# Turning rows by VectorE blocks and a way through DRAM, in place of TensorE transposes, in a kernel's last FFN

## The chip, the cores and the metric

The kernel runs on one core of a Trainium2 chip, as one program. A core has a matrix engine (TensorE, PE in the profile, with its weight loads PEld), three elementwise engines (VectorE = DVE, ScalarE = ACT, GpSimd = POOL), a queue engine (SyncE, SP) that issues most transfers, and 16 DMA engines that move data between HBM (device DRAM) and the on-chip memory SBUF, which has 128 partitions. TensorE writes its results to PSUM, eight banks of 128 x 512 float32 here. Each engine runs its own instructions in order and waits for the others by semaphores. The metric is the device time of one execution in microseconds (us); a kernel's time is the median of its runs.

## What is computed

Eight sequences of 512 rows with 512 features pass through four layers, each with a residual and a layer norm behind it: causal attention with 16 heads, a mixture of eight experts with two chosen for each row, attention with 8 heads over 2 groups of keys, and an FFN with integer weights. The change lies in that last FFN:

```python
def _L1_ffn_ref(x, wq_gate, s_gate, wq_up, s_up, wq_down, s_down):
    DIM = 512
    HID = 1408
    ZERO_POINT = 128.0

    def _qlinear(x, wq, scale):
        W = (wq.astype(jnp.float32) - ZERO_POINT) * scale[:, None]
        return jnp.einsum('bsd,hd->bsh', x, W)
    gate = _qlinear(x, wq_gate, s_gate)
    gate = jax.nn.silu(gate)
    up = _qlinear(x, wq_up, s_up)
    return _qlinear(gate * up, wq_down, s_down)
...
x = _layernorm(x + _L1_ffn_ref(x, L1_ffn_wq_gate, L1_ffn_s_gate, L1_ffn_wq_up, L1_ffn_s_up, L1_ffn_wq_down, L1_ffn_s_down), axis=-1)
```

For each sequence the FFN takes 512 x 512 rows to a hidden width of 1408 and back.

## The kernel before

The program runs the four layers one after the other; what follows is about the last, class `IntegerFfn`, and what surrounds it. P = 128 is the number of partitions, NB = 8 the number of sequences ("batches"), S = D = 512, NT = 4 tiles of 128 rows, ND = 4 tiles of 128 features, NHID = 11 chunks of 128 hidden features.

**Where the rows are.** `env.xs[b]` holds batch b in SBUF with the rows on the partitions: `[128, NT, 512]`, row 128 t + p on partition p of tile t. A matmul contracts over the partitions, so gate and up need the features there: x has to be turned. That is `split` (L1013). For feature tile c it turns four 128 x 128 squares by TensorE into one PSUM bank, `ps_xT` (L1022), ScalarE copies the bank to `x_high` in float32r, a type that TensorE takes in one pass and that keeps fewer bits (L1023), and VectorE subtracts that from the bank, which gives the rest, `x_low` (L1024). The two halves together stand for x. They lie in the pool `rows` for even batches and in the pool `work` for odd ones, one buffer each; so the halves of batch b + 2 take the room of batch b's.

**A chunk.** `hidden` (L1047) makes chunk c of a batch: 8 matmuls for the gate into `ps_g` and 8 for up into `ps_u` (L1055: 4 feature tiles, 2 halves), Silu by ScalarE (`sg`, L1058), product and scale by VectorE (`hT`, L1060), then the halves of hT: the copy `h_half` high by ScalarE (L1063) and the rest, `h_half` low, by VectorE (L1064). `out` (L1067) multiplies a chunk's halves by the down weights and adds it into four banks `ps_f` (L1069: 4 row tiles, 2 halves, 8 matmuls). `ps_g` and `ps_u` have two banks each, `ps_f` four: all eight. `ps_xT` takes a bank of `ps_g`.

**A batch.** `batch` (L1080) runs through the 11 chunks; behind chunk c's gate and up comes chunk c - 1's `out`, so that VectorE and ScalarE have the time of the next gate and up for their part. In chunks 2 to 5 it calls `split` for one feature tile each of the next batch:

```python
if not final and 2 <= c < 2 + ND:
    self.split(b + 1, c - 2, self.p_gu.tile([P, S], F32, tag="g", name="ps_xT"))
```

After chunk 10 `scaled` (L1072) applies the output scales (`y_ffn`, L1075) and the residual (L1076), and `layernorm` (L143) makes statistics (L148, L149), a power on GpSimd (L150, L151) and the normalised rows (L153), and stores them by four DMAs of 256 KB on SP (L156). The last batch ends by another way, `last_rows`.

Batch 0's rows are turned before that, inside the attention, whose plan calls `split` four times. `run` (L1026) opens the pools, loads and converts the rest of the integer weights (L980, L994, with a check of their size, L926), while batch 0 runs, and then runs the batches.

**What sets the order.** The attention's order is written by hand. In the FFN a scheduler orders each engine's instructions by priority and readiness; instructions may stand ahead of others that the source has earlier. At a batch's end, for instance, the next batch's gate and up stand ahead of parts of what the source puts first.

Of the kernel before, what the change touches and what calls it, by code (L numbers as in the profile page):

```python
# [18 lines left out]
P = 128  # L19
NB = 8  # L20
# [43 lines left out]
class Inputs:  # L64
# [3 lines left out]
    def __init__(self, *aps):  # L68
        for name, ap in zip(self.names, aps, strict=True):
            setattr(self, name, ap)  # L70


class Env:
# [928 lines left out]
class IntegerFfn:  # L1002
# [2 lines left out]

    HELD = 4

    def __init__(self, env, guard, weights, rows):
        self.env, self.nc, self.guard, self.weights, self.rows = env, env.nc, guard, weights, rows
        self.halves = {}  # L1010

    def split(self, b, c, ps):


        nc = self.nc
        if c == 0:
            pool = self.work if b % 2 else self.rows
            self.halves[b] = [pool.tile([P, ND, S], F32R, tag=f"rows{i}", name=f"x3_{part}")
                              for i, part in enumerate(("high", "low"))]
        high, low = self.halves[b]  # L1020
        for t in range(NT):
            nc.tensor.transpose(ps[:, ts(t, P)], self.env.xs[b][:, t, ts(c, P)], self.env.ident)  # L1022
        nc.scalar.copy(high[:, c, :], ps)  # L1023
        nc.vector.tensor_tensor(low[:, c, :], ps, high[:, c, :].bitcast(F32), ALU.subtract)  # L1024

    def run(self, held_out, last_norm):  # L1026
        tc, nc, weights = self.env.tc, self.nc, self.weights
        with ExitStack() as phase:
            self.work = phase.enter_context(tc.tile_pool(name="d_work", bufs=1))
            self.p_gu = phase.enter_context(tc.tile_pool(name="d_gu", bufs=2, space=PSUM))  # L1030
            self.p_o = phase.enter_context(tc.tile_pool(name="d_o", bufs=1, space=PSUM))
            weights.open(phase.enter_context(tc.tile_pool(name="d_weights", bufs=1)), 3 * NHID - weights.at)
            self.sd = self.work.tile([P, D], F32, name="sd")
            with tc.tile_pool(name="d_slots", bufs=1) as slots:
                while weights.at < 3 * NHID:
                    weights.load(slots, 4, 3 * NHID)
                    weights.convert()
                nc.sync.dma_start(out=self.sd, in_=self.env.ins.s_down.partition_broadcast(P))
            self.late = phase.enter_context(tc.tile_pool(name="d_late", bufs=self.HELD))
            for b in range(NB):  # L1040
                self.batch(b)
                if b == 0:
                    last_norm()
                    ps = self.p_gu.tile([1, 1], F32, tag="g", name="ps_held")
                    nc.scalar.dma_start(out=held_out, in_=self.guard.partitions_held(self.env.const, ps))

    def hidden(self, b, c, held):  # L1047

        nc, vec, work, weights = self.nc, self.env.vec, self.work, self.weights
        g = self.p_gu.tile([P, S], F32, tag="g", name="ps_g1")  # L1050
        u = self.p_gu.tile([P, S], F32, tag="u", name="ps_u1")
        for ps, w in ((g, weights(2 * c)), (u, weights(2 * c + 1))):
            for dc in range(ND):
                for i, x in enumerate(self.halves[b]):
                    nc.tensor.matmul(ps, lhsT=w[:, ts(dc, P)], rhs=x[:, dc, :],  # L1055
                                     start=(dc, i) == (0, 0), stop=(dc, i) == (ND - 1, 1))
        sg = work.tile([P, S], F32, tag="sg", name="sg1", bufs=2)
        nc.scalar.activation(sg, g, AF.Silu, scale=vec[:, V_SG + c : V_SG + c + 1])  # L1058
        hT = work.tile([P, S], F32, tag="hT", name="hT2", bufs=2)
        nc.vector.scalar_tensor_tensor(hT, u, vec[:, V_SU + c : V_SU + c + 1], sg, ALU.mult, ALU.mult)  # L1060
        high, low = (self.late.tile([P, S], F32R, tag=f"h{i}", name="h_late") if held else
                     work.tile([P, S], F32R, tag=f"h{i}", name="h_half", bufs=2) for i in range(2))
        nc.scalar.copy(high, hT)  # L1063
        nc.vector.tensor_tensor(low, hT, high.bitcast(F32), ALU.subtract)  # L1064
        return high, low

    def out(self, os, t, c, parts):  # L1067
        for i, h in enumerate(parts):
            self.nc.tensor.matmul(os[t], lhsT=h[:, ts(t, P)], rhs=self.weights(2 * NHID + c),  # L1069
                                  start=(c, i) == (0, 0), stop=(c, i) == (NHID - 1, 1))  # L1070
# [8 lines left out]
    def batch(self, b):  # L1079
        env, nc = self.env, self.nc  # L1080
        os = [self.p_o.tile([P, D], F32, tag=f"o{t}", name=f"ps_f{t}") for t in range(NT)]
        final = b == NB - 1
        hold = NHID - self.HELD if final else NHID
        parts = {}
        for c in range(NHID):
            parts[c] = self.hidden(b, c, c >= hold)
            if 0 < c <= hold:
                for t in range(NT):
                    self.out(os, t, c - 1, parts[c - 1])

            if not final and 2 <= c < 2 + ND:
                self.split(b + 1, c - 2, self.p_gu.tile([P, S], F32, tag="g", name="ps_xT"))
        if not final:
            for t in range(NT):
                self.out(os, t, NHID - 1, parts[NHID - 1])
            for t in range(NT):
                self.scaled(b, os, t)
            env.layernorm(b, env.ins.out[b])
            return

        order = [(t, c) for ts_ in ((0, 1), (2,), (3,)) for cs in (range(hold, NHID - 1), (NHID - 1,)) for t in ts_ for c in cs]
        for t, c in order:
            self.out(os, t, c, parts[c])
            if c == NHID - 1:
                self.last_rows(b, t, self.scaled(b, os, t))
# [587 lines left out]
def usual_pass(tc, ins, held_out):  # L1693
    nc = tc.nc
    with ExitStack() as ctx:
        env = Env(ctx, tc, ins)
        guard = Guard(env)
        keep = ctx.enter_context(tc.tile_pool(name="routed", bufs=1, side="right"))
        dram = ctx.enter_context(tc.tile_pool(name="routed_rows", bufs=1, space=bass.MemoryType.DRAM))
        with tc.tile_pool(name="a_mm", bufs=2, space=PSUM) as p_mm, ExitStack() as attn1_ctx:  # L1700
            with tc.tile_pool(name="routes", bufs=1, side="right") as routes, \
                    tc.tile_pool(name="experts", bufs=1, side="right") as pool, ExitStack() as tiles_ctx:
                experts = Experts(env, pool)
                router, tiles, tables = attention0(env, guard, keep, routes, experts, dram, p_mm, tiles_ctx)

                def load_rows(b):
                    rows = router.rows[S * b : S * (b + 1)]
                    nc.sync.dma_start(out=env.xs[b], in_=rows.rearrange("(t p) d -> p t d", p=P))

                env.open_stream(ctx, range(NB // 2))  # L1710
                rows = ctx.enter_context(tc.tile_pool(name="c_rows", bufs=1))
                own = attn1_ctx.enter_context(tc.tile_pool(name="c_own", bufs=1))
                attention = Attention1(env, guard, router, rows, own, p_mm)
                beside = {tiles.next + 6 * (b + 1): lambda b=b: load_rows(b) for b in range(NB // 2)}

                for i, piece in enumerate(attention.first_pieces()):
                    beside[E * NT + 4 + 2 * i] = piece
                with in_order(tc):
                    while tiles.next < tiles.n:
                        tiles.step()  # L1720
                        next(tables, None)
                        beside.pop(tiles.next, lambda: None)()
                assert not beside and next(tables, None) is None
                tiles.rare()
            env.open_stream(ctx, range(NB // 2, NB), side="right")
            for b in range(NB // 2, NB):
                load_rows(b)
            weights = IntegerWeights(env, guard)
            weights.open(ctx.enter_context(tc.tile_pool(name="c_weights", bufs=1, side="right")), weights.FIRST)
            ffn = IntegerFfn(env, guard, weights, rows)  # L1730
            last_norm = attention.run(weights, ffn.split)
        ffn.run(held_out, last_norm)

# [305 lines left out]
```

## Time and profile before

| | us |
|---|---|
| median of 3 runs | 2284.05 (2281.4 to 2284.93) |
| the profiled execution | 2286.21 |
| its span, first to last instruction | 2284.5 |
| last FFN, first gate matmul to the end | 1766.8 to 2284.5 |
| granted TensorE clock, mean over the span | 0.995 |
| transposes `ps_xT` (L1022), all batches | 128 of 272 ns, busy 19.2 |
| copies `x_high` (L1023) | 32 of 587 ns |
| subtractions `x_low` (L1024) | 32 of 689 ns |

The profile is of one execution. Engines are named PE, PEld, DVE, ACT, POOL and SP; L12 is line 12 of the kernel. A row of a group gives line, engine, operation, the output and the inputs by their names, shapes and the count, then the busy time of all and the mean of one in ns, then the idle time of that engine just before them and what ended it. The chain of waits goes back from the last instruction to whatever released it. Matmul durations overlap each other, since matmuls are pipelined; what a matmul costs on the path is the distance from start to start.

### The profile page before, as it was taken

What the parts mean: (1) busy time and instruction counts of PE and PEld (TensorE: products, weight loads), DVE (VectorE), ACT (ScalarE), POOL (GpSimd) and SP (SyncE); (2) the same over time, 40 slices, a digit from 0 to 9 for tenths busy, and PEclk for the clock granted to TensorE, in tenths of its full rate; (3) what the DMA queues carried; (4) which work ended last, traced back from release to release, by engine and by line L of the source; (5) the groups of instructions that cost most, each with busy time, mean ns of one, the idle gap of its engine ahead of it and who ended that gap; (6) DMA issues with size and microseconds to landing.
All of it is one profiled execution on the core that took longest, in us unless ns stands there. A gap on an engine that the chain in (4) does not pass through costs nothing. (4 is left out here: it accounts for less than half of the span.)

```text
span 2284.5 us, 24183 instructions
## 1 busy us (share of the span) xinstructions
PE 2238.4 (98%) x9430; PEld 1153.0 (50%) x9430; DVE 1242.0 (54%) x1976; ACT 648.2 (28%) x937; POOL 496.2 (22%) x489
## 2 busy tenths in 40 slices
PE   9999999999998999999999999999999999999997
PEld 3344444444443444444443334443343777887776
DVE  3457576566657433242216877787667544444443
ACT  2332322323323221111223323333332222222222
POOL 2232423313233241131115122322211000000000
PEclk9999999999999999999999999999999999999999
DMA  8010101101112224232224011100100100000000
GB/s 290 19 56 1 56 19 37 56 1 56 47 45 74 93 85 174 91 125 88 92 84 147 10 56 56 49 27 27 37 1 17 48 19 19 19 19 19 19 19 20
DMA packets 58444, 126.63 MB, mean 55 GB/s; under 512 B 6210, under 2 KB 6210, under 8 KB 58322
## 3 DMA queue, kind: packets, MB, share of 16 engines
q1 hardware_dynamic: 47040, 89.32, 11.1%
q0 software_dynamic: 10560, 34.61, 5.2%
q8 instruction: 77, 1.26, 0.2%
q10 hardware_dynamic: 722, 1.07, 0.1%
q14 instruction: 45, 0.37, 0.0%
HBM read 89.59 MB, written 35.39 MB: 55 GB/s over the span
## 5 line engine op out<-in xcount | busy, mean ns | idle before, releaser
L845 PE MATMUL ps_gu<-experts,xrT 128*128 128x512 f32 (+1 forms) x520 | 248.7, 601 | 0.0
L1268 ACT ACTIVATE p<-sc 128x2048 f32<-128x2048 f32 (+1 forms) x96 | 152.9, 1593 | 189.0 <-PE sc L1264 189.0
L1273 POOL TENSOR_SCALAR_AFFINE_SELECT p<-p 128x512 f32<-128x512 f32 x128 | 93.2, 743 | 380.1 <-ACT p L1268 374.0
L1060 DVE SCALAR_TENSOR_TENSOR hT<-ps_u,vec,sg 128x512 f32<-128x512 f32 x88 | 65.8, 748 | 198.4 <-PE ps_u L1055 198.4
L1069 PE MATMUL ps_f<-ffn_w,h_half 128*128 128x512 f32 x672 | 169.8, 393 | 1.6 <-DVE h_half L1064 1.1
L934 POOL TENSOR_TENSOR g_total<-g_total,r_inv 128x512 f32<-128x512 f32 x64 | 89.7, 1402 | 359.7 <-DVE r_inv L1617 283.3
L1617 DVE RECIPROCAL r_inv<-r_inv 128x512 f32<-128x512 f32 x32 | 106.9, 3339 | 97.5 <-ACT r_inv L931 97.5
L1587 ACT ACTIVATE p<-sc 128x1024 f32<-128x1024 f32 x128 | 124.0, 1021 | 125.9 <-PE sc L1584 125.9
L1296 DVE TENSOR_TENSOR p<-p 128x1536 f32<-128x1536 f32 (+2 forms) x96 | 129.2, 1345 | 38.7 <-POOL p L1273 21.7
L1069 PEld LDWEIGHTS ps_f<-ffn_w,h_half 128*128 128x128 f32 x672 | 124.3, 188 | 34.9 <-DVE h_half L1064 7.6
L1055 PE MATMUL ps_g<-x_high,ffn_w 128*128 128x512 f32 x352 | 141.0, 401 | 0.8 <-DVE x L1558 0.8
L848 DVE TENSOR_TENSOR h<-ps_gu,h 128x256 f32<-128x256 f32 x67 | 28.4, 423 | 205.6 <-ACT h L847 205.6
L1055 PE MATMUL ps_g<-x_low,ffn_w 128*128 128x512 f32 x352 | 139.0, 395 | 0.0
L1055 PE MATMUL ps_u<-x_low,ffn_w 128*128 128x512 f32 x352 | 138.8, 394 | 0.0
L1055 PE MATMUL ps_u<-x_high,ffn_w 128*128 128x512 f32 x352 | 138.6, 394 | 0.0
L862 PE MATMUL ps_y<-experts,hT 128*128 128x512 f32 (+1 forms) x272 | 127.9, 593 | 0.5 <-ACT hT L856 0.5
L1584 PE MATMUL sc<-qT,kT 64*128 64x512 f32 x512 | 127.2, 615 | 1.0 <-ACT qT L1505 0.7
L1200 PE MATMUL ps_q<-experts 128*128 128x512 f32 x256 | 121.2, 615 | 4.3 <-DMA experts<-in_xT 4.3
L845 PEld LDWEIGHTS ps_gu<-experts,xrT 128*128 128x128 f32 x520 | 89.6, 192 | 68.2 <-issue 68.1
L1606 PE MATMUL av<-p,v 128*64 128x512 f32 x512 | 123.7, 605 | 0.0
L1193 PE MATMUL ps_v<-experts 128*128 128x512 f32 x256 | 116.3, 602 | 2.1 <-DVE v L1195 2.1
L1552 PE MATMUL ps_o<-attn_out,aoT 128*128 128x512 f32 x256 | 117.3, 602 | 0.8 <-ACT r_inv L931 0.8
(256 smaller groups left out, 3532.3 us busy)
## 6 DMA issues: line engine op xcount, KB each, us to landing
results<-y SPq DMA_DIRECT2D x68, 256.0 KB, 2.0
x<-in_x SPq DMA_DIRECT2D x8, 1024.0 KB, 7.5
experts<-in_gate_up SPq DMA_DIRECT2D x8, 1024.0 KB, 11.7
rows<-x SPq DMA_DIRECT2D x32, 256.0 KB, 2.1
x<-rows SPq DMA_DIRECT2D x8, 1024.0 KB, 11.3
experts<-in_xT SPq DMA_DIRECT2D x7, 1024.0 KB, 5.5
out<-x SPq DMA_DIRECT2D x28, 256.0 KB, 2.3
ffn_i<-in_wq_ffn SPq DMA_DIRECT2D x11, 512.0 KB, 4.3
```

The source lines that it names most:

```text
L845: mm = nc.tensor.matmul(ps, lhsT=xT[:, c, :], rhs=self.weights(i, c), start=c == 0, stop=c == ND - 1)
L862: self.nc.tensor.matmul(ps, lhsT=hT[:, c, :], rhs=self.weights(i, ND + c), start=c == 0, stop=c == self.NI - 1)
L1055: nc.tensor.matmul(ps, lhsT=w[:, ts(dc, P)], rhs=x[:, dc, :], start=(dc, i) == (0, 0), stop=(dc, i) == (ND - 1, 1))
L1069: self.nc.tensor.matmul(os[t], lhsT=h[:, ts(t, P)], rhs=self.weights(2 * NHID + c), start=(c, i) == (0, 0), stop=(c, i) == (NHID - 1, 1))
L1193: nc.tensor.matmul(ps, lhsT=xts[b][:, c, ts(t, P)], rhs=wv[:, c, :], start=c == 0, stop=c == ND - 1)
L1200: nc.tensor.matmul(ps, lhsT=wq[:, g, ts(c, P)], rhs=xts[b][:, c, :], start=c == 0, stop=c == ND - 1)
L1268: nc.scalar.activation(p, sc[:, :, :width], AF.Exp, scale=scale)
L1296: nc.vector.tensor_tensor(total[:, :, P * kt :], total[:, :, P * kt :], p[:, :, at : at + w], ALU.add)
L1552: nc.tensor.matmul(ps, lhsT=state[b]["aoT"][:, c, ts(t, P)], rhs=w_out[:, c, :], start=c == 0, stop=c == ND - 1)
L1584: nc.tensor.matmul(sc[:, j, :], lhsT=st["kT"][hs, ts(kt, P)], rhs=st["qT"][g][hs, :], start=True, stop=True)
L1587: nc.scalar.activation(p, sc, AF.Exp, scale=scale)
L1606: nc.tensor.matmul(st["av"][HD * j : HD * (j + 1), :], lhsT=st["v"][:, kt, HD * j : HD * (j + 1)], rhs=p[:, j, :], start=kt == 0, stop=kt ...
```

## The change

In the last FFN the rows of batches 1 to 7 no longer go over TensorE. A new class `Turn` turns them in two steps. `blocks` has VectorE turn each square of 32 x 32 by itself, one instruction for a row tile of 128 x 512, from `xs` into `turned`. That leaves the squares themselves in the wrong partitions. `out` stores the tile to a DRAM buffer by four DMAs on SP, each from 32 partitions, with runs of 128 floats, so that the squares change places; `back` loads the buffer by one DMA of 1,024 KB, 8 KB on each partition. Both use the same SBUF tile `turned`, in a pool of one buffer. There are two DRAM buffers, for even and odd batches.

The rows' order along the free dimension then is (block of 32, tile, row in the block) in place of (tile, row). Gate, up, Silu and product run on columns in that order; the two instructions that make the halves of hT put them in order again, by reading hT through a permuted view (`by_tile`). Batch 0 is turned as before.

`split` is now `parts` for batches 1 to 7: the copy and the subtraction read `turned` in SBUF and not PSUM. In `batch`, chunks 0 to 3 call `blocks` for one row tile each of the next batch (the fourth also issues the five DMAs), chunks 6 to 9 call `parts`. The pool of the last batch's held halves, `late`, is opened only after the pool of `turned` is closed.

```diff
+class Turn:
+    N = P // 32
+
+    def __init__(self, env, dram, n, name):
+        self.nc, self.n = env.nc, n
+        self.dram = dram.tile([P, ND, self.N, n * 32], F32, name=name)
+
+    def blocks(self, room, t, x):
+        out = room.rearrange("p (j t c) -> p j t c", t=self.n, c=32)[:, :, t, :]
+        self.nc.vector.transpose(out, x.rearrange("p (j c) -> p j c", c=32))
+
+    def out(self, room):
+        for i in range(self.N):
+            src = room[32 * i : 32 * (i + 1), :].rearrange("r (k j f) -> r k j f", j=self.N, f=self.n * 32)
+            self.nc.sync.dma_start(out=self.dram.rearrange("(j r) k i f -> r k j i f", j=self.N)[:, :, :, i, :], in_=src)
+
+    def back(self, room):
+        self.nc.sync.dma_start(out=room, in_=self.dram.rearrange("p k i f -> p (k i f)"))
+
+    def by_tile(self, a, turned):
+        if turned:
+            return a.rearrange("p (i t c) -> p t i c", i=self.N, c=32)
+        return a.rearrange("p (t i c) -> p t i c", i=self.N, c=32)
...
 class IntegerFfn:
...
+        self.turns = [Turn(env, dram, NT, f"turned_{i}") for i in range(2)]
...
+    def room(self, b):
+        pool = self.work if b % 2 else self.rows
+        self.halves[b] = [pool.tile([P, ND, S], F32R, tag=f"rows{i}", name=f"x3_{part}")
+                          for i, part in enumerate(("high", "low"))]
+
+    def blocks(self, b, t):
+        if t == 0:
+            self.room(b)
+            self.turned = self.raw.tile([P, ND * S], F32, tag="turned", name="turned")
+        turn = self.turns[b % 2]
+        turn.blocks(self.turned, t, self.env.xs[b][:, t, :])
+        if t == NT - 1:
+            turn.out(self.turned)
+            turn.back(self.turned)
+
+    def parts(self, b, c):
+        high, low = (half[:, c, :] for half in self.halves[b])
+        x = self.turned[:, ts(c, S)]
+        self.nc.scalar.copy(high, x)
+        self.nc.vector.tensor_tensor(low, x, high.bitcast(F32), ALU.subtract)
...
+            with tc.tile_pool(name="d_raw", bufs=1) as self.raw:
+                for b in range(NB - 1):
+                    self.batch(b)
...
             self.late = phase.enter_context(tc.tile_pool(name="d_late", bufs=self.HELD))
...
+            self.batch(NB - 1)
...
-        nc.scalar.copy(high, hT)
-        nc.vector.tensor_tensor(low, hT, high.bitcast(F32), ALU.subtract)
+        hT, *halves = [self.turns[0].by_tile(a, back) if b else a for a, back in ((hT, True), (high, False), (low, False))]
+        nc.scalar.copy(halves[0], hT)
+        nc.vector.tensor_tensor(halves[1], hT, halves[0].bitcast(F32), ALU.subtract)
...
-            if not final and 2 <= c < 2 + ND:
-                self.split(b + 1, c - 2, self.p_gu.tile([P, S], F32, tag="g", name="ps_xT"))
+            if not final and c < NT:
+                self.blocks(b + 1, c)
+            if not final and 0 <= c - 6 < ND:
+                self.parts(b + 1, c - 6)
```

More of the change, by code (lines that the diff above doesn't have):

```diff
@@ L1006, with __init__ @@
     HELD = 4
-    def __init__(self, env, guard, weights, rows):
+    def __init__(self, env, guard, weights, rows, dram):
         self.env, self.nc, self.guard, self.weights, self.rows = env, env.nc, guard, weights, rows
         self.halves = {}
+        self.turns = [Turn(env, dram, NT, f"turned_{i}") for i in range(2)]
[17 more added lines that the diff above has]
+        self.nc.vector.tensor_tensor(low, x, high.bitcast(F32), ALU.subtract)
     def split(self, b, c, ps):
@@ L1016, in split @@
         if c == 0:
-            pool = self.work if b % 2 else self.rows
-            self.halves[b] = [pool.tile([P, ND, S], F32R, tag=f"rows{i}", name=f"x3_{part}")
-                              for i, part in enumerate(("high", "low"))]
+            self.room(b)
         high, low = self.halves[b]
@@ L1038, in run @@
                 nc.sync.dma_start(out=self.sd, in_=self.env.ins.s_down.partition_broadcast(P))
-            self.late = phase.enter_context(tc.tile_pool(name="d_late", bufs=self.HELD))
[L1040 to L1045, printed above, removed]
+            with tc.tile_pool(name="d_raw", bufs=1) as self.raw:
+                for b in range(NB - 1):
+                    self.batch(b)
+                    if b == 0:
+                        last_norm()
+                        ps = self.p_gu.tile([1, 1], F32, tag="g", name="ps_held")
+                        nc.scalar.dma_start(out=held_out, in_=self.guard.partitions_held(self.env.const, ps))
+            self.late = phase.enter_context(tc.tile_pool(name="d_late", bufs=self.HELD))
+            self.batch(NB - 1)
     def hidden(self, b, c, held):
@@ L1729, in usual_pass @@
             weights.open(ctx.enter_context(tc.tile_pool(name="c_weights", bufs=1, side="right")), weights.FIRST)
-            ffn = IntegerFfn(env, guard, weights, rows)
+            ffn = IntegerFfn(env, guard, weights, rows, dram)
             last_norm = attention.run(weights, ffn.split)
```

## The prediction

> **What bounds the kernel now.** I read the busy shares first, then the stretches of the last FFN, one batch each, then the chain of waits inside one batch, then the costliest groups, the waits and the DMA rows.
>
> The page's busy shares:
>
> ```profile
> PE 2238.4 (98%) x9430; PEld 1153.0 (50%) x9430; DVE 1242.0 (54%) x1976; ACT 648.2 (28%) x937; POOL 496.2 (22%) x489
> ```
>
> Two stretches of the last FFN (time, busy time of each engine, granted clock, DMA share):
>
> ```profile
> core 0: us, PE busy (x) PEld busy (x) DVE busy (x) ACT busy (x) POOL busy (x), PEclk, DMA share, GB/s
> 1894.00:1958.00 64.00, 63.81 (x284) 51.31 (x283) 28.38 (x48) 16.77 (x26) 1.27 (x2) 1.00 0.05 17
> 1958.00:2021.00 63.00, 62.82 (x280) 50.53 (x279) 27.43 (x47) 16.77 (x26) 1.27 (x2) 1.00 0.05 17
> ```
>
> TensorE, 98% busy over the span, is busy for all but 0.2 us of each stretch, at full granted clock; VectorE is busy 44%, ScalarE 26%, the DMA engines 5%. So time taken from TensorE's stream is time off the end, as long as nothing else in a batch comes to exceed it.
>
> The chain of waits from batch 4 (counted from 0) into the next (start, length, what):
>
> ```profile
> 2021.44 1.88 PE ps_g L1055 x8
> ...
> 2034.94 1.81 PE ps_f L1069 x8
> 2036.75 0.44 PE ps_xT L1022 x4
> 2037.19 1.85 PE ps_g L1055 x8
> 2039.04 1.86 PE ps_u L1055 x8
> 2040.90 1.82 PE ps_f L1069 x8
> 2042.72 0.44 PE ps_xT L1022 x4
> ...
> 2060.62 1.87 PE ps_g L1055 x8
> 2062.49 1.86 PE ps_u L1055 x8
> 2064.35 1.82 PE ps_f L1069 x8
> 2066.17 1.87 PE ps_g L1055 x8
> ...
> 2084.82 1.88 PE ps_g L1055 x8
> ```
>
> The transposes stand on the path. A chunk with them takes 2043.15 - 2037.19 = 5.96 us (2043.15 is the end of the second group), one without 2066.17 - 2060.62 = 5.55. A batch takes 2084.82 - 2021.44 = 63.4.
>
> **The change, part by part.** *Removed from TensorE:* 16 transposes in each of seven batches, in 28 groups of four. A group is 0.44 by the chain, 0.41 to 0.42 by the difference of chunks; I take 0.43: 28 x 0.43 = **12.0 us**. Their matmul row (272 ns each, modelled ends) would give 30; those overlap, so the chain decides. Batch 0's four groups still go over TensorE, inside the attention.
>
> The rows that price what moves (busy, mean ns | idle before):
>
> ```profile
> L1060 DVE SCALAR_TENSOR_TENSOR hT<-ps_u,vec,sg 128x512 f32<-128x512 f32 x88 | 65.8, 748 | 198.4 <-PE ps_u L1055 198.4
> L1064 DVE TENSOR_TENSOR h_half<-hT,h_half 128x512 fp32r<-128x512 f32 x84 | 57.5, 691 | 46.1 <-ACT h_half L1063 46.1
> L1063 ACT CAST h_half<-hT 128x512 fp32r<-128x512 f32 x84 | 52.1, 621 | 154.0 <-DVE hT L1060 154.0
> ```
>
> *Halves of x.* Still four copies and four subtractions a batch, now from SBUF: as L1063 and L1064, 0.62 and 0.69 us (from PSUM 0.587 and 0.689). No change of load.
>
> *Block transposes.* Four of 128x512 a batch on VectorE. No row shows this operation. Bounds: 0.48 us (L153, four in 1.92) and 3.34 (the reciprocal, L1617, the dearest VectorE operation of this size). It has one input, one output and no arithmetic, so it is nearest to the simple ones: I take 0.69, 2.8 us a batch. The cover is VectorE's idle 35 us in 63; in one chunk of 5.55 it has 1.44 of its own work. In the built order they stand in most batches after chunk 2's hT, two ahead of chunk 2's low half and two behind it. That half is due some 4.6 us after hT; two blocks and the half take 2.1. Batch 0 is tightest: integers are converted there, the four blocks stand before chunk 4's hT and follow a conversion that waits for its load until 1789.48 and a reduction. I work out the low half ready at about 1796.8 against 1797.5 due. Nothing is lost; at double the price 2 us.
>
> The Trainium skill (VectorE: DVE Perf Modes, Rules for kernel authors) says to turn 128x128 on TensorE wherever PSUM will do, which speaks against this change, and in The three transpose paths gives 311 ns for VectorE's blocks of 128x128 bf16. Four of those would be 1.24 us a tile, an estimate; by it the sum would be about 10 us of gain in place of 12. No run so far shows the operation.
>
> *The way through DRAM.* Five DMAs a batch on SP: four writes of 256 KB, each from 32 partitions in runs of 512 B, then a load of 1,024 KB that waits for all four. Rows near and far (KB each, us from issue to landing):
>
> ```profile
> x<-rows SPq DMA_DIRECT2D x8, 1024.0 KB, 11.3
> out<-x SPq DMA_DIRECT2D x28, 256.0 KB, 2.3
> ffn_i<-in_wq_ffn SPq DMA_DIRECT2D x2, 1024.0 KB, 5.3
> attn_out<-in_w_attn SPq DMA_DIRECT2D x2, 512.0 KB, 17.4
> ```
>
> Packets of 2,048 B on this queue last 84 ns (median of the trace's packet records). The writes are 2,048 packets, 128 on each of 16 engines: 2.7 us if a quarter of the bytes takes a quarter of the time, 10.8 if a packet costs the same whatever its size; with 2.3 for a landing, 5 to 13. The load takes 5.3 to 11.3. Round trip 10 to 25 us; I take 16. The far bound is the row from 64 partitions: 2 x 17.4 + 11.3 = 46.
>
> Who waits for it: the copies x_high on ScalarE, behind them that chunk's h_half, behind that ps_f on TensorE. The lead, by the built order: rows of batches 3 to 7 are turned two batches ahead, at chunk 2, and split after chunk 10's gate and up (the halves' room is then free): seven chunks, 39 us. Batch 1's are turned before chunk 4 of batch 0 and split after chunk 8's Silu: 18 us, and 4 more before TensorE lacks anything. Batch 2's are turned after chunk 8 of batch 0 and split after chunk 2's Silu of batch 1: 20 us, under 1 of grace. At 16 all is hidden. On SP the load's wait holds back only the 256 KB writes of finished rows, for which nobody waits.
>
> *Between batches.* Here an edit isn't free. In batches 1 to 5 three x_high (1.86 us) now stand ahead of chunk 10's h_half on ScalarE, three x_low ahead of its low half on VectorE. Today the stretch from chunk 9's ps_f to chunk 1's loses 0.78 us by the timeline: 16 ps_f in 3.95 in place of 3.64, 0.35 in ps_u, 0.12 in the next ps_f. In the built order two gate matmuls (0.47) stand before the ps_f that needs the high half: it comes 2.75 us after chunk 9's ps_f begins, is due after 2.29, and a weight load comes first: a stall of 0.6. The low half is in time. ps_f then ends late, so the VectorE chain behind it (y_ffn, x, statistics, norm, chunk 0's low half) moves by 1.5 us; the built order asks for that half some 1.4 us later than before, leaving 0.1. So 0.7 in place of 0.8: nothing. Bounds: -0.8 a boundary, and +1.3 if the moved chain isn't absorbed, over five boundaries -4 to +6.5.
>
> *Permuted reads.* Columns of seven batches come in another order, and L1063's copy and L1064's subtraction put them right by reading hT in runs of 32. No row shows such a read; bounds once and twice the price. I take once: as many elements, one pass. Within a batch either is covered by 3 us of slack between the low half and its ps_f.
>
> **Sum.** The profiled execution took 2286.21 us (span 2284.5 and 1.7 around it), 2.2 above the median of the runs, 2284.05. 2286.2 - 12.0 = 2274.2 for it; on the median **2272**.
>
> **The rivals.**
> 1. *The first two turns land late.* At a round trip of 25 us the first costs 3 and the second 4: 2279. For: short runs, 32 partitions. Against: DMA engines at 5% and four 256 KB writes landing in 2.7 us together (packets from 1968.02 to 1970.76). 0.09.
> 2. *The turn through DRAM is slower than its lead; slower than before.* Beyond 22 us each microsecond costs up to two (both early turns), so from 27 us the 12 are gone, from 30 the kernel is measurably slower, and beyond 39 every batch stalls. At the far bound of 46: 24 + 25 + 5 x 7 = 84, 2356; at 35 us, 2299. For: the attn_out row. Against: that row and x<-rows wait behind other traffic in a busier part; here the queue is idle. 0.06. The Trainium skill (VectorE: DVE Perf Modes, The three transpose paths) warns that a plain DMA with strides for a transpose is 19 times slower than the crossbar's when the innermost stride is large; here the innermost run is 512 B in one piece, so by its own condition it would not apply. No run so far shows it.
> 3. *Permuted reads cost double.* 0.62 and 0.69 more on h_half's two steps: between batches, where there is no slack, the first ps_f waits 1.2, the chain behind moves on, 2.35 lost in place of 0.7: 1.65 x 7 = 11.5, 2283.5, no change. For: runs of 128 B. Against: nothing in the page. 0.07.
> 4. *Blocks at 3.34 us:* 13.4 a batch in two bursts. Two blocks ahead of the low half make ps_f wait 2.9, the next two 3.3, in five batches 31; in batch 0, 10 and 8: 49 lost, 2321. 0.04.
> 5. *More than 12:* the stalls between batches vanish (-4): 2268. 0.04.
>
> **How the numbers follow.** The forecast has 0.70, own range 2269 to 2277. Measured changes below 0.2% (4.6 us) can't be told from none, so faster means under 2279.5, slower over 2288.6. Faster: forecast 0.70, rival 5 0.04, half of rival 1 0.04: 0.78. Same: the other half 0.05 and rival 3 0.07: 0.12. Slower: rivals 2 and 4: 0.10. The range 2266 to 2283.5 reaches over rivals 5, 1 and 3 and leaves out 2 and 4 and the edges.
>
> **What would show it.** Right: no ps_xT after batch 0's; chunks of 5.55 us throughout; batches of about 61.7; 28 block transposes near 0.7 us; the load landed well before x_high. Wrong: ScalarE or VectorE waiting for the load of turned (rivals 1, 2, worst at the first two); L1063's and L1064's successors above 0.7 (rival 3); ps_f waiting for h_half over 1 us between batches.

## The result and the profile after

| | before | after |
|---|---|---|
| median, us | 2282.77 (2281.4 to 2284.93, 4 runs) | 2269.44 (2267.03 to 2271.88, 4 runs) |
| profiled execution and its span, us | 2286.21, 2284.5 | 2270.12, 2268.4 |
| last FFN, first gate matmul to the end | 1766.78 to 2284.49: 517.72 | 1764.29 to 2268.36: 504.08 |
| from one batch to the next, batches 3 to 6 | 63.38 to 63.39 | 61.34 to 61.39 |

The ratio is 0.9941, 95% interval 0.9924 to 0.9958: 13.3 us faster. Within the two traces the last FFN alone is 517.72 - 504.08 = 13.64 us shorter. It begins 2.5 us earlier as well, but its start lay anywhere from 1761.3 to 1767.6 us in the traces of this study. So I read the stage by itself.

Busy shares of the changed kernel:

```profile
PE 2224.5 (98%) x9318; PEld 1142.3 (50%) x9318; DVE 1257.6 (55%) x2004; ACT 645.4 (28%) x937; POOL 494.5 (22%) x489
```

TensorE has 112 matmuls fewer, VectorE 28 instructions more. A stretch of the last FFN, about one batch (time, busy time of each engine, granted clock, DMA share):

```profile
1886.00:1948.00 62.00, 62.00 (x269) 49.76 (x267) 30.13 (x52) 17.05 (x29) 1.26 (x2) 1.00 0.16 51
```

The DMA share is 0.16 in place of 0.05, and TensorE has no idle time left that shows here. Groups of the last FFN (busy us, mean ns of one | idle before, and what ended it):

```profile
L1122 DVE TENSOR_TENSOR h_half<-hT,h_half 128x512 fp32r<-128x512 f32 x84 | 57.3, 688 | 37.1 <-ACT h_half L1121 37.1
L1121 ACT CAST h_half<-hT 128x512 fp32r<-128x512 f32 x84 | 52.1, 620 | 147.5 <-DVE hT L1116 147.5
...
L88 DVE STREAM_TRANSPOSE turned<-x 128x512 f32<-128x512 f32 x28 | 17.8, 682 | 0.0
L1066 ACT CAST x_high<-turned 128x512 fp32r<-128x512 f32 x28 | 15.9, 618 | 4.2 <-PE ps_u L1111 4.2
```

A block transpose of 128x512 float32 takes 682 ns. The halves of hT, which now read runs of 32, cost what they did (688 against 691, 620 against 621; batch 0's eleven chunks, read in plain order, take 688 and 621, the other batches 686 to 691 and 619 to 621). ScalarE's copies never waited for the load of `turned`: what ended their idle time is `ps_u`.

The DMA rows (KB each, us from issue to landing) and SP's timeline over batch 0 (start, length, what):

```profile
turned<-turned SPq DMA_DIRECT2D x28, 256.0 KB, 3.9
turned<-turned SPq DMA_DIRECT2D x7, 1024.0 KB, 4.8
```

```profile
1791.72 3.25 SPq L93 DMA_DIRECT2D turned<-turned  x4
1798.33 0.36 SPq L96 DMA_DIRECT2D turned<-turned  x1
1817.53 3.22 SPq L93 DMA_DIRECT2D turned<-turned  x4
1824.14 0.34 SPq L96 DMA_DIRECT2D turned<-turned  x1
```

From the first write's issue to the load's is 6.6 us, and the load takes 4.8: a round trip of 11.4. The copies that use it began at 1810.69 and 1838.07, 19.0 and 20.5 us after the first write; for later batches it is 39 to 41.

The chain of waits from batch 2 into batch 3 (start, length, what):

```profile
by line: PE ps_f L1127 35.6%; PE ps_u L1111 32.7%; PE ps_g L1111 32.2%
...
1946.05 1.82 PE ps_f L1127 x8
1947.87 0.47 PE ps_g L1111 x2
1948.34 0.95 PE ps_f L1127 x4
1949.29 0.24 PE ps_g L1111
1949.53 1.03 PE ps_f L1127 x4
1950.56 1.17 PE ps_g L1111 x5
```

In this window, from 1944 to 2012 us, nothing but TensorE stands on the chain. Before, the same stretch between two batches ran over `y_ffn`, the statistics, the power on GpSimd and the normalisation; this is the kernel before from batch 3 into batch 4:

```profile
2017.49 3.95 PE ps_f L1069 x16
2021.44 1.88 PE ps_g L1055 x8
2023.33 0.68 DVE y_ffn L1075
...
2030.00 1.92 DVE x L153 x4
2031.92 0.61 DVE h_half L1064
2032.58 1.20 PE ps_f L1069 x4
```

Chunk 10's ps_f is now split, and gate matmuls of the next batch stand in the gaps.

Between batches 3 and 6 a batch takes 2.03 us less. Four groups of transposes at 0.43 are 1.7 of that; the remaining 0.3 is what the stretch between batches lost before and no longer loses. Over 28 groups and five boundaries that is 12.0 + 1.6, the 13.6 of the stage. This split is by subtraction. Adding up what the starts of matmuls around a boundary lie apart beyond their usual 230 ns (where it is over 245) gives 0.75 us before and 0.34 after, so 0.4 a boundary and 2.1 in all; the two ways differ by half a microsecond, and nothing here says which is nearer.

The other periods can't be compared one by one: 64.26, 63.40 and 63.40 before, 62.58, 59.50 and 63.49 after, for batches 0, 1 and 6. At the boundaries into batches 1 and 7 the changed kernel has the order of before, with all sixteen ps_f ahead of the next gate, and loses 0.73 and 0.75 as before. At the five between them, eight ps_f (1.8 us) come after the next batch's first gate matmul, so batch 1's period is short by them and batch 6's long.

### The profile page after: what moved, and what is told of

Read it like the earlier page. It is cut to its first block, busy times and chain, and to the rows that moved or that the text cites. A ratio compares the mean times of both kernels' runs of the same rounds, so it can differ in the third digit from the quotient of the medians.

```text
span 2268.4 us, 24071 instructions
## 1 busy us (share of the span) xinstructions
PE 2224.5 (98%) x9318; PEld 1142.3 (50%) x9318; DVE 1257.6 (55%) x2004; ACT 645.4 (28%) x937; POOL 494.5 (22%) x489
## 3 DMA queue, kind: packets, MB, share of 16 engines
q1 hardware_dynamic: 62832, 104.01, 13.6%
```

## The experiments

Stage means the last FFN from its first gate matmul to the end, in one trace. Medians are compared with runs of the kernel before on the same chip; those were 2283.4 us in the first four runs, 2284.58 in the next four, 2285.43 in the next three and 2286.05 beside the last.

### What a group of transposes costs

```diff
-        for t in range(NT):
+        for t in [*range(NT)] * (2 if b else 1):
             nc.tensor.transpose(ps[:, ts(t, P)], self.env.xs[b][:, t, ts(c, P)], self.env.ident)
```

> The kernel before, with each of the 28 groups of four TensorE transposes of batches 1 to 7 done twice into the same PSUM tile. Theory (a group costs the path its own 0.43 us, 12.0 us in all): 2294 to 2296 us, against 2282.8 before. Rival (the groups partly filled idle time of TensorE, and the gain came from elsewhere): 2290 us or less.

Measured: 2297.92 us, ratio 1.0060 (1.0046 to 1.0073), 14.5 us more than before and 1.9 above the range. The stage is 530.54 us, 12.8 more, and a batch 65.23 in place of 63.38, 1.85 for four groups: 0.46 a group. In the chunk differences of the kernel before it was 0.41. So a group costs 0.41 to 0.46 us in the chunks where it stands, none of it fills a gap, and 28 of them are 11.5 to 12.9 us. The stage is the cleaner number of the two: nothing was changed ahead of it, and what comes ahead of it differs from execution to execution by more than the 1.7 us between 14.5 and 12.8.

### What the turn costs while it is hidden

The block transposes and all DMAs are taken out; the halves read the rows as they lie.

```diff
-            self.turned = self.raw.tile([P, ND * S], F32, tag="turned", name="turned")
-        turn = self.turns[b % 2]
-        turn.blocks(self.turned, t, self.env.xs[b][:, t, :])
-        if t == NT - 1:
-            turn.out(self.turned)
-            turn.back(self.turned)
...
-        x = self.turned[:, ts(c, S)]
+        x = self.env.xs[b][:, c, :]
```

> The changed kernel without the whole turn: no block transposes on VectorE, no writes to DRAM and no loads back; the copies and subtracts that make the halves of x read the rows of batches 1 to 7 as they lie, so the rows of those batches enter the last FFN unturned. TensorE's instructions are the changed kernel's. Theory (28 block transposes of 0.68 us and seven round trips of 11.4 us lie wholly beside TensorE's work): the changed kernel's time within 1.5 us, 2268 to 2271 us, with periods of 61.3 us between batches as there. Rival (the hidden work costs something after all, through VectorE's 19 us or through a DMA share of 0.17 in place of 0.05): faster than the changed kernel by 3 us or more, 2266 us or less.

Measured: 2266.35 us (2264.29 to 2270.83), ratio 0.9930 (0.9917 to 0.9944). The median lies 1.65 below the theory's range and close to the rival's bound; by times alone it decides nothing, since the interval overlaps the changed kernel's. The stage does: 503.13 us, 0.95 less than the changed kernel's 504.08, and all of it is in the first two batches, 59.76 + 61.12 in place of 62.58 + 59.50. From batch 2 on the periods are 61.35 to 61.39, against 61.34 to 61.39. There the turn is free. In batch 0 the two kernels also differ in order: without the load to wait for, batch 1's copies are made as the FFN starts, and two normalisations no longer stand ahead of hT of chunk 0. So the 0.95 is not the turn's price. Most of it goes with the order: the kernel further down that turns batch 0 as well keeps every block and transfer and has 59.66 + 60.93 there, with only some 0.4 of the difference due to faster matmuls of two chunks (see there).

### The stretch between batches

As the run before, and `halves[b]` is batch 0's for all batches, so copies and subtracts go as well:

```diff
-            self.room(b)
...
+            self.halves[b] = self.halves[0]
...
-            if not final and 0 <= c - 6 < ND:
-                self.parts(b + 1, c - 6)
```

> The kernel of the run without the turn, and without the copies and subtracts that make the halves of x in batches 1 to 7 as well: all eight batches read batch 0's halves. The order that is built then has, between two batches, the sixteen matmuls of chunk 11's ps_f in a row, as before the change, and no gate matmuls of the next batch among them. Theory (of the 13.3 us gained, 12.0 are TensorE's own transposes, and the rest are stalls between batches that shrank from 0.78 to 0.4 us because gate matmuls of the next batch stand among those of ps_f): the stalls come back, 0.7 us in place of 0.4 at each of five boundaries, 1.5 to 2.5 us slower than the run without the turn: 2270 to 2272.5 us. Rival (the boundary got shorter because the TensorE transposes left it, and the order is nothing; or ScalarE's and VectorE's copies and subtracts, 1.3 us a tile, cost something): equal to the run without the turn, or faster, 2269.5 us or less.

Measured: 2272.18 us, ratio 0.9948 (0.9934 to 0.9961): 5.8 us slower than the run without the turn, with less work, where I had expected 1.5 to 2.5. The single runs of the two touch (2270.28 to 2272.89 against 2264.29 to 2270.83), so the stage is the surer number: 506.22, 3.1 more, and the periods 61.71 in place of 61.36. The rival falls. The chain of that kernel from batch 2 into batch 3:

```profile
1947.03 1.66 PE ps_f L1121 x6
1948.69 1.88 PE ps_g L1105 x8
...
1950.58 0.68 DVE y_ffn L1127
...
1957.25 1.92 DVE x L185 x4
1959.17 0.61 DVE h_half L1116
...
1959.83 1.20 PE ps_f L1121 x4
```

That is the chain of the kernel before again, through `y_ffn` and the normalisation to the low half that the first ps_f of the next batch waits for. The 0.35 us that a boundary loses more comes with that order and goes with the other one. No run changes only the order. But two boundaries of the same kernels bear it out: the one into batch 7 has the order of before in the changed kernel and loses what it lost (0.75), and the one into batch 1, which has the new order in the run without the turn and in the kernel that turns batch 0 too, loses 0.23 there in place of 0.73. The rest of the 5.8 us is not in the stage, and is not explained.

### The changed kernel again

> The changed kernel as it is, for a time from the same chip as the three runs beside it, and for a second look at what varies between executions. Theory (the stage of the last FFN, from its first gate matmul to the end, is set by TensorE's own work, and what differs between executions lies ahead of it): that stage 503.5 to 504.6 us again (504.08 in the first trace), the time 2267 to 2272 us. Rival (the stage itself varies by a microsecond or more): a stage outside 503 to 505 us; the 0.95 us by which the run without the turn was shorter there would then say nothing.

Measured: 2271.13 us (2269.6 to 2272.85), ratio 0.9942 (0.9929 to 0.9955); stage 504.33.

> The changed kernel once more, beside the two runs of this call: 2268 to 2272 us, its last stage 503.5 to 504.6 us, as in both traces so far (504.08 and 504.33).

Measured: 2272.35 us, just above the range, ratio 0.9938 (0.9925 to 0.9951); stage 504.03. Three traces of the stage agree within 0.3 us, while its start varies from 1764.3 to 1767.6. The ratios agree within 0.0004.

### A slower block transpose

```diff
-        turn.blocks(self.turned, t, self.env.xs[b][:, t, :])
+        for _ in range(5):
+            turn.blocks(self.turned, t, self.env.xs[b][:, t, :])
```

> The changed kernel with each block transpose done five times over into the same place, 5 x 0.68 = 3.4 us a tile, which is the upper bound of the prediction for one. VectorE gets 28 x 4 x 0.68 = 76 us more in the last FFN, where it is idle for more than 30 us of each batch's 61 us; the built order has twenty in a row behind chunk 3 of batch 0, and spreads the others over the chunks. Theory (hidden where VectorE has room within its chunk; the twenty in a row, 13.6 us, are paid but for the 2.7 us that four took and a chunk's slack): 8 to 11 us more than the changed kernel, all in batch 0, periods of 61.3 to 62 us afterwards: 2276 to 2283 us. Rival, as the prediction priced tiles of 3.34 us: 49 us more than its forecast, 2321 us. Rival (wholly hidden): within 2 us of the changed kernel.

Measured: 2275.76 us (2272.55 to 2277.44), ratio 0.9960 (0.9946 to 0.9974), 4.6 us more than the changed kernel beside it, half of what I had expected; stage 509.09, 4.8 more. The periods are 65.34, 62.54, 62.43, 60.52, 60.36, 61.35, 63.51. VectorE's timeline in batch 0 (start, length, what):

```profile
1790.35 11.97 DVE L88 STREAM_TRANSPOSE turned<-x 128x512 f32<-128x512 f32 x20
1802.25 1.36 DVE L1117 SCALAR_TENSOR_TENSOR hT<-ps_u,vec,sg 128x512 f32<-128x512 f32 x2
```

Twenty in a row hold VectorE for 12 us, and two chunks' hT come together behind them. TensorE has the gate matmuls of two chunks in a row meanwhile, sixteen of them, and so waits only 3.2 us of the 12. Another 1.7 are lost behind the wait: from 1803.0 to 1807.2 the granted clock is 0.59 on average, and the first matmuls start 427 ns apart. In all, 76 us of added VectorE work cost 4.8. These are five short instructions that others can come between, not one long one as in rival 4.

### A longer way through DRAM

The write and the load are done twice, and in another run four times:

```diff
-            turn.out(self.turned)
-            turn.back(self.turned)
+            for _ in range(2):
+                turn.out(self.turned)
+                turn.back(self.turned)
```

> The changed kernel with the write to DRAM and the load back done twice for each batch, one after the other; after an even number the rows of batches 1 to 7 stand in another order, so the last FFN gets them unturned. The way through DRAM then takes 2 x 11.4 = 22.8 us. The order that is built has the copies of the halves of batch 1 at the end of batch 0 and those of later batches ever later, with leads of some 39 us from the first write to the copy. Theory (the way is hidden as long as it is shorter than its lead, and twice the DMA traffic, a share of 0.3 in place of 0.17, costs TensorE nothing): the changed kernel's time within 2 us, 2268 to 2272 us; the copies wait for no load. Rival (DRAM traffic in itself slows TensorE's stage, or the copies wait): 2275 us or more, with waits for the load ahead of the copies.

Measured: 2279.76 us, ratio 0.9978 (0.9968 to 0.9988), 8.6 more than the changed kernel beside it; stage 511.61, 7.5 more (less 504.08). The theory's time fell, and the rival's cause is not what happened. The second load was issued at 1809.20 and the copies began at 1822.67, behind chunk 10's `h_half` and not behind a load; the period of batch 1 alone is 67.96, of batches 4 and 5 60.55 and 60.36. One stretch there, and what TensorE waited for between 1790 and 1850 us (total us, times, longest):

```profile
2077.00:2137.00 60.00, 60.00 (x260) 48.37 (x259) 28.09 (x49) 15.13 (x25) 1.27 (x2) 1.00 0.28 88
```

```profile
PEld ps_g L1112 <- DVE x_low L1068: 4.7, 1, 4.7
```

With a DMA share of 0.28 TensorE is busy without a gap in this stretch, so the traffic costs it nothing there. By the starts of matmuls, 6.4 of the 7.5 us are one boundary, where the order built for this kernel put batch 1's four subtractions on VectorE behind `y_ffn`, the residual and a statistic, and the first gate matmuls of batch 1 wait for them: 4.4 us of waiting, and 1.5 more because the next seven start some 427 ns apart and not 230, at a granted clock of 0.52 (1830.2 to 1833.3). At the three boundaries after it, the order of before is back and loses 0.72 to 0.75 each.

> As the run with two ways through DRAM, with four, 46 us in all, the far bound of the prediction; the rows stand in another order again. The order that is built has the copies and subtracts for batch 1 after chunk 10 of batch 0, and for every batch right ahead of its first gate matmul, behind the four y_ffn and the normalisation on VectorE. Theory (a late turn costs what TensorE waits for its last half of x, and no more): batch 1's load lands at 1791.7 + 46 = 1838 us, 11 to 12 us after its first gate matmul is due, and each of the other six boundaries costs 3 to 7 us, since four subtracts of 0.69 us stand behind VectorE's four y_ffn of 0.7 us there: 30 to 54 us together, 2300 to 2324 us. Rival, as the prediction priced it (each batch's copies stand in ScalarE's order 39 us behind the write and every one of seven waits): 2356 us. Rival (no cost, since the planner moves the copies): under 2280 us.

Measured: 2415.76 us, ratio 1.0582 (1.0566 to 1.0599); stage 646.33, 142 more. All three forecasts were far too low. Periods are 79.5 to 90.2 us. SP's timeline at one boundary, and SP's waits over the stage (total us, times, longest):

```profile
2051.23 3.22 SPq L93 DMA_DIRECT2D turned<-turned  x4
2084.00 1.55 SPq L188 DMA_DIRECT2D out<-x  x3
2085.72 0.46 SPq L96 DMA_DIRECT2D turned<-turned  x1
```

```profile
SPq L188 <- DVE x L185: 194.6, 9, 30.9
```

The chain there (start, length, what):

```profile
2085.72 6.16 DMA turned<-turned
...
2091.90 0.63 ACT x_high L1067
...
2092.57 4.08 PE ps_g L1112 x8
```

The fourth set of writes was issued from 2051.23 on; the load belonging to it was issued only at 2085.72. In between SP stood at `out<-x`, the stores of the batch's finished rows, which wait for the normalisation at the batch's end. Then the load took its 6.2 us, then came the copy, then the first gate matmul of the next batch; the eight gate matmuls take 4.08 us where they take 1.87 elsewhere. SP takes its instructions in order; a wait there is a wait for everything behind it. To test that, the 28 stores were moved to POOL's queue and nothing else changed:

```diff
-            env.layernorm(b, env.ins.out[b])
+            env.layernorm(b, env.ins.out[b], self.nc.gpsimd)
```

> The run with four ways through DRAM, with the 28 stores of the finished rows issued from POOL's queue in place of SP's; nothing else differs, and the orders of VectorE and ScalarE stay. With SP's queue, each batch's last load stood behind four stores that waited for the end of the batch's normalisation, so that the load (6.2 us) and the first copy came after it, and a boundary lost 18.6 to 19.8 us. Theory (a late load on SP is a matter of what stands before it in SP's order): the last load lands during chunk 9 or 10, and a boundary loses only VectorE's chain of y_ffn, statistics and normalisation that stands before the first subtract, 11 to 13 us; at the first one the load is late as well. Six boundaries times 6 to 8 us less: 2360 to 2375 us against 2415.8. Rival (the four ways are themselves too slow, by DRAM or by traffic): 2405 us or more, with the first gate matmul waiting for the copy behind the load at every boundary.

Measured: 2369.98 us, ratio 1.0373 (1.0358 to 1.0388), inside the theory's range; stage 601.53 in place of 646.33, 44.8 less, 6.4 for each of seven boundaries on average. At the boundaries into batches 2 to 7 it now loses 12.3 to 13.6 us, by VectorE's order:

```profile
1990.69 1.00 DVE x L185 x2
1991.69 0.61 DVE x_low L1068
...
1992.35 3.30 PE ps_g L1112 x7
1995.65 1.87 PE ps_u L1112 x8
```

Some 10.5 us of that are the wait for the first subtraction behind the normalisation; most of the rest is the slow pace of the matmuls behind it, seven in 3.30 us. No load is waited for there; only at the first boundary do the copies still wait for one, 21.1 us. So of the 142 us that four ways cost, 44.8 are the stores on SP, and most of the rest is the wait that VectorE's order makes, with the slow pace behind it.

### Batch 0 as well

```diff
-    FIRST = 20
+    FIRST = 16
...
-        hT, *halves = [self.turns[0].by_tile(a, back) if b else a for a, back in ((hT, True), (high, False), (low, False))]
+        hT, *halves = [self.turns[0].by_tile(a, back) for a, back in ((hT, True), (high, False), (low, False))]
...
-                for c, i in enumerate((0, 2, 4, 6)):
-                    todo[i].append(lambda c=c: split(0, c, self.mm([P, S], "ps_xT")))
+                todo[0].append(split)
+                for c, i in enumerate((4, 5, 6, 7)):
+                    todo[i].append(lambda c=c: split(c))
```

Here `split` without a chunk turns all four tiles and issues the DMAs, with one it makes that tile's halves; the room of `turned` in attention comes from holding 16 units of integer weights early and not 20.

> The changed kernel with batch 0 turned in the same way, during the last batch of attention, so that its four groups of four TensorE transposes go too; more integer weights are loaded and converted in batch 0 of the FFN to make room. Theory (a group of four costs TensorE 0.43 us wherever it stands, and the new way is hidden): 4 x 0.43 = 1.7 us less than the changed kernel, 2267 to 2268.5 us. Rival (that part of attention has other stalls that TensorE's transposes fill, or the conversions of batch 0 delay its chunks): the same or slower, 2269.5 us or more.

Measured: 2266.99 us (2266.06 to 2267.8), just below the range, ratio 0.9926 (0.9912 to 0.9940); stage 501.50.

> The kernel that turns batch 0 in the new way too, once more beside the changed kernel on one chip. Theory (four groups of 0.43 us less in attention, and a batch 0 of the last FFN whose copies for batch 1 stand between its matmuls of ps_f, which gave a stage of 501.50 us in place of 504.08): 2.5 to 4.5 us less than the changed kernel beside it, its stage 501 to 502 us. Rival (the 2.9 us between the medians of two calls were the chip's or chance): within 1.5 us of it.

Measured: 2266.18 us (2264.46 to 2268.17), ratio 0.9920 (0.9907 to 0.9932), 6.2 us less than the changed kernel beside it at 2272.35, more than the 2.5 to 4.5 expected; stage 501.64, 2.4 less. This is the fastest kernel that computes everything, in two sets of runs that agree. The gain is not all the four groups: 2.4 us of it lie in the FFN. There batch 0 loses 0.6 us between its matmuls in place of 1.4, and chunks 8 and 9, whose weights now lie in the second block, run their gate and up matmuls in 227 ns from start to start and not 234: 2 x 16 x 8 x 6.5 ns = 1.7. How much of the rest is the groups in attention can't be told, as the start of the stage varies by more than 1.7 us.

### Why 234 and 227

```diff
         self.parts += [(pool.tile([P, n, 512], F32R, name=f"ffn_w{len(self.parts)}"), n)]
+        if len(self.parts) == 1:
+            pad = pool.tile([P, 24], F32, name="pad")
+            self.env.nc.gpsimd.memset(pad, 0.0)
```

> The kernel that turns batch 0 too, with one edit more: an unused tile of 96 bytes a partition beside the first block of the integer weights, which starts that block at byte 163200 of a partition, a multiple of 128, in place of 163296, which is 32 above one. Ground: in every trace so far a gate or up matmul whose weights lie in that block starts 233.5 ns after the one ahead of it, and one whose weights lie in the second block (at byte 108800, a multiple of 128) 227 ns after; with the block cut from 20 units to 16, chunks 8 and 9 went over from 233.5 to 227. Theory (where the weights start within a line of SBUF sets these 6.5 ns): all gate and up matmuls at 227 ns, 8 chunks x 16 matmuls x 8 batches x 6.5 ns = 6.7 us less than the same kernel without the edit, a stage of 494.5 to 496 us in place of 501.6, 2258.5 to 2261.5 us. Rival (it is the part of SBUF or the tile, and not its start): 233.5 ns as before, a stage of 501 to 502 us, 2265 to 2268 us.

Measured: 2267.66 us, ratio 0.9924 (0.9911 to 0.9936); stage 502.10. Chunks 0 to 7 stand at 231 to 232 ns by the median, 8 to 10 at 227 as before. By the mean they went only from 233.3 to 232.5, and the down matmuls of chunks 3 and 5 slowed from 227 to 231, so none of the time went. Starting the block at a multiple of 128 bytes does not bring 227; what does stays open.

## Why the prediction was right, and where it was not

- *Removed transposes, 12.0 us:* right. Doubling them gave 12.8 in the stage; in the trace before, the starts around the 28 groups add up to about 12.0.
- *Halves, no change; permuted reads at once the price:* right, 618 and 685 ns for the halves of x (0.62 and 0.69 were taken), 620 and 688 for those of hT. Rival 3 is out.
- *Block transposes at 0.69 us, hidden:* right, 0.68. Rival 4's condition did not come about, and five times the work costs nothing like its 49 us: the kernel pays 4.8, because the scheduler spreads the blocks over the chunks from batch 1 on, and in batch 0 TensorE takes gate matmuls first. One instruction of 3.4 us was not tried. The Trainium skill (VectorE: DVE Perf Modes, The three transpose paths) led to an estimate of 1.24 us a tile from its 311 ns for 128x128 bf16; the trace has 0.68 for four times that width in float32, so the measurement decides. The Trainium skill's rule to turn 128x128 on TensorE where PSUM will do (VectorE: DVE Perf Modes, Rules for kernel authors) does not hold for time on this kernel, where TensorE is 98% busy and VectorE 55%: 13.3 us went the other way.
- *Way through DRAM, 16 us, leads of 18, 20 and 39:* the leads were right (19.0, 20.5, 39 to 41), the trip shorter, 11.4. Nothing waited, so rival 1 is out.
- *Between batches, "So 0.7 in place of 0.8: nothing":* this is the mis-sized term. It measured -0.3 to -0.4 a boundary, -1.6 to -2.1 in all, within the bounds given and in the direction of rival 5, whose stalls shrank (0.75 to 0.34) but did not vanish. The step that failed in it is the stall of 0.6 at the high half. ScalarE's timeline there:

```profile
1945.86 1.66 ACT L1066 CAST x_high<-turned 128x512 fp32r<-128x512 f32 x3 [0.84 <-PE ps_u L1111]
1947.43 0.61 ACT L1121 CAST h_half<-hT 128x512 fp32r<-128x512 f32 x1
```

The three copies hold ScalarE for 1.57 us until the next begins, 0.52 each, not 1.86: back to back they overlap. They began 0.2 ahead of chunk 9's ps_f, and h_half was done at 1948.04, 1.99 after that ps_f began and 0.3 before it was needed, where I had 2.75 and too late.

- *Rival 2, lateness priced by the lead alone:* not met by the change, but the price was wrong. "On SP the load's wait holds back only the 256 KB writes of finished rows, for which nobody waits" looked in one direction. In the other, the stores hold back the load, and 44.8 us of the 2415.8 came from that. The price also took the order as fixed: with four ways the order that is built puts the subtractions behind the normalisation, and with the stores off SP the time is still 2370, above the 2356 forecast for 46 us.

The forecast of 2272 against 2269.44 is off by 2.6 us. Half of that is the gain, 13.3 in place of 12.0, which the one term covers; the other half is the median of before, 2284.05 in three runs and 2282.77 in four. The gain did not come from anywhere that the prediction had not named.

## What to carry to other kernels

Work taken off an engine that is never idle is worth its start-to-start time in the chain, and doubling it is the cleanest way to show that. Work moved to idle engines is free only in the order that gets built: the same kernel with less work was slower (no copies), and with more transfers it lost 6 us at one boundary through an order, and 142 in all through an order and a queue, of which the queue was 45. So for each transfer on a queue ask not only how long it takes but which waiting instruction stands ahead of it.

## What the hardware showed unexpectedly

- ScalarE's copies of 128x512 last 0.62 us each in the rows, but begin 0.52 us apart when nothing is between them; VectorE's block transposes last 0.68 and begin 0.59 apart.
- A write of 256 KB from 32 partitions in runs of 512 B holds SP for 0.64 us (median of 28) against 0.33 for the load of 1,024 KB, and lands in 3.9 us where stores of whole rows took 2.3.
- The same gate and up matmuls follow each other in 227 or 234 ns, by the block of SBUF that holds their weights, in every trace but the last. Cutting the first block moved two chunks from one to the other; starting it at a multiple of 128 bytes changed the median from 234 to 232 and the mean by 0.8. The cause wasn't found.
- Where TensorE had waited 3 us or more in the last FFN (3.2 in the run with five blocks, 4.4 with two ways, 10.5 and more with four), its next matmuls started 427 ns apart in place of 230, with a granted clock of 0.5 to 0.6 in those stretches. This added 1.5 to 3 us to each such wait. Behind waits of 0.6 us and less it does not show.
- In the profiled run with four ways the mean granted clock was 0.968, and 0.978 with the stores on POOL's queue, against 0.992 to 0.997 in the runs of the others.
